# Reordering the opening and the first phase of a Mamba mixer: half of the step sizes under the down projection, four scores, B's and C's transposes and x's taps at other places

## The chip, the core and the metric

The kernel runs on one core of a Trainium2 chip. The core has five engines with a queue each, which run their instructions in order and wait for one another by semaphores: TensorE (PE; its weight loads are listed as PEld) for matmuls into the accumulation memory PSUM, VectorE (DVE) and ScalarE (ACT) for elementwise work, GpSimd (POOL) for elementwise work[...], and SyncE (SP), which here only issues the DMA transfers between the chip's main memory and the on-chip buffer. The metric is the device time of one execution in microseconds (us), lower is better.

## What is computed

Four residual blocks in a row on x, 1024 tokens of width 512 in two sequences of 512: a block-sparse linear layer, a gated feed-forward block (FFN) with dequantized weights, a Mamba-2 mixer, and the same FFN again. Each begins with a layer norm. The change is in the mixer and at the seam of the first FFN and the mixer. Cut to what matters (H = 128 heads of 64, 8 groups of B and C with 128 states, chunks of 128 tokens; the function's name is shortened):

```python
def mixer_ref(hidden_states, ...):
    proj = hidden_states @ in_proj_w.T          # gate 8192 | x 8192, B 1024, C 1024 | dt 128
    hBC = silu(causal_conv4(hBC) + conv_b)      # 4 taps along the tokens
    dt = jax.nn.softplus(dt + dt_bias)          # the step sizes
    A_dt = -jnp.exp(A_log) * dt
    x_dt = x * dt[..., None]
    A_cumsum = jnp.cumsum(Ac, axis=-1)          # within each chunk
    Lmat = jnp.exp(segment_sum(Ac))             # decay between two tokens of a chunk
    Gm = jnp.einsum('bclhn,bcshn->bclsh', Cch, Bch)
    M = Gm * Lmat                               # the scores
    Y_diag = einsum(M, x_dt)
    states = einsum(Bch * decay_states, x_dt)   # then carried from chunk to chunk
    Y_off = einsum(Cch, states) * exp(A_cumsum)
    y = (Y_diag + Y_off) + D * x
    y = y * rsqrt(mean(y * y) + EPS) * norm_w * silu(gate)
    return y @ out_proj_w.T
```

## The kernel before

**Order.** For PE, ACT and DVE the order of instructions is the order in which the program writes them; for POOL and SP a planner sets it from the same text, by what it expects to be ready. A small generator is the tool by which the text interleaves work: `seven` yields after each of seven products, and the caller puts other work between `next(steps)` calls.

**Projections.** A pair of 128-column weight tiles times all 1024 tokens is computed as a Strassen-like scheme, `seven` (L157): seven products instead of eight, each of two 128-deep steps of float32, 4 PE instructions. It needs sums of quarters of the tokens (`quarters`, L138, and `last_quarter`, L143: two subtractions on DVE, two on POOL, the last one in place) and sums of weight quarters (`left_sides`, four POOL instructions for each load of a pair). Its three PSUM banks x, y, z are written more than once: y by the second, fourth and sixth product. Between them DVE adds y to a temporary (L180, L185, L186, L194, L199), and the next product into y waits until that has read it. The finished quarters go to `done`, in the mixer to `conv` (L551): ACT writes bias and last tap (L553), and three DVE instructions, the taps (L556), are put on a list that `drain(n)` empties later. They read the PSUM bank, so it is in use until then.

**The seam.** The FFN ends with the down projection (L404): eight rows of 128 tokens, 28 PE instructions each. After each row, `to_mixer` (L1094) stores the row and starts its norm, and two rows later `turn` (L123) transposes it with four PE instructions into `xn_t`.

**The mixer's opening** (L777 on). `step_sizes` (L456) multiplies the tokens by the dt weights (`pre`, 32 PE instructions a sequence) and takes softplus in seven DVE and four ACT instructions over both sequences at once; `decays` (L503) makes the cumulative sums with a triangular matrix of ones, sends them to main memory (`acs_d`), and keeps copies and the chunk decays. The order of `before` on PE: step sizes of sequence 0, the last two tile transposes, step sizes of sequence 1, x of the first pair of tiles (seven products), B and C of group 0 (seven, in the banks of tag `yo`), `decays`, the gate of the first pair (seven). Then the silus.

**A phase** (L854) handles two tiles of 128 channels, 4 heads, in both sequences: four units (tile j, sequence b), of two heads each. It projects the next pair's x (`x_front`) and gate (`g_front`) while it finishes the present pair: `tokens` transposes x and multiplies by dt (L652, L656, and L660 on POOL), `group_scores` (L590; for a new group only) transposes B and makes C times B, masked, in `gm`; `scores` (L705) makes one head's exponentials of the sums (ACT: four L712, L719, L722) from a broadcast of `acs_d` (`load_sums`, L620), multiplies them by C on POOL (L723), and puts the multiplication by `gm` (L720, DVE) on a list that `flush` empties. `both_states` makes the states (L673 and five DVE instructions a unit), `half_scan` the outputs (L731, L740), `gated` (L750, L751) multiplies by the gate. `outs` multiplies the pair before last by the output weights (L765), eight times in a phase; phase 1 has nothing to multiply yet. Scores are numbered 0 to 7; two of the next pair's are made at the end of each phase, but in phase 1 of `before` all eight of the present pair are made in the phase itself. There are 31 such phases and a tail.

Of the kernel before, what the change touches and what calls it, by code (L numbers as in the profile page):

```python
# [24 lines left out]
G = 8  # L25
# [12 lines left out]
def kernel(  # L38
# [98 lines left out]

    def quarters():  # L138
        nc.vector.tensor_sub(tq[:, 0], B12, B11)
        nc.vector.tensor_sub(tq[:, 1], B22, tq[:, 0])  # L140
        nc.gpsimd.tensor_sub(tq[:, 2], B21, tq[:, 1])
# [177 lines left out]
    def ffn(which, first, waiting, after):  # L319
# [3 lines left out]
        with tc.tile_pool(name=f"ffn{which}", bufs=1) as pool:  # L323
# [80 lines left out]
            for t in range(NT):  # L404
                po = psum.tile([P, DIM], F32, tag="proj", name="ffn_o", bufs=3)
                for fc in range(NFC):
                    nc.tensor.matmul(  # L407
                        po,
                        lhsT=h_t[:, fc, t * P : (t + 1) * P],
                        rhs=down[:, fc, :],  # L410
                        start=(fc == 0),
                        stop=(fc == NFC - 1),
                    )
                nc.vector.tensor_add(x_sb[:, t, :], x_sb[:, t, :], po)
                after(t)


    def mixer(waiting):

        with ExitStack() as st:  # L420
# [13 lines left out]
            dt = sc.tile([P, NT, H], F32, tag="dt", name="dt")  # L434
            acs = sc.tile([P, NT, H], F32, tag="acs", name="acs")
# [9 lines left out]
            w_dt = weights()[:, :, 0, :]  # L445
            nc.sync.dma_start(
                w_dt, win_t[:, 2 * INTER + 2 * G * P :].rearrange("(kc p) h -> p kc h", p=P)
            )
            row = const.tile([P, 2, H], F32, name="row")
            dtb, aneg = row[:, 0, :], row[:, 1, :]  # L450
            nc.sync.dma_start(dtb, dt_bias.to_broadcast([P, H]))
            nc.sync.dma_start(aneg, a_log.to_broadcast([P, H]))
            nc.scalar.activation(aneg, aneg, AF.Exp)
            nc.vector.tensor_scalar(aneg, aneg, -1.0, None, ALU.mult)

            def step_sizes(wdt, pool):  # L456

                v = pool.tile([P, NT, H], F32, tag="bc", name="v", bufs=3)

                def pre(b):  # L460
                    pd = psum.tile([P, NCH, H], F32, tag="tr", name="pd")
                    for c in range(NCH):
                        t = b * NCH + c
                        for kc in range(KC):
                            nc.tensor.matmul(
                                pd[:, c, :],
                                lhsT=xn_t[:, kc, t * P : (t + 1) * P],
                                rhs=wdt[:, kc, :],
                                start=(kc == 0),
                                stop=(kc == KC - 1),  # L470
                            )
                    nc.vector.tensor_tensor(
                        v[:, b * NCH : (b + 1) * NCH, :],
                        pd,
                        dtb.unsqueeze(1).to_broadcast([P, NCH, H]),
                        ALU.add,
                    )

                e = pool.tile([P, NT, H], F32, tag="bc", name="e", bufs=3)
                u = pool.tile([P, NT, H], F32, tag="bc", name="u", bufs=3)
                pre(0)
                yield
                pre(1)
                nc.scalar.activation(e, v, AF.Abs)
                nc.scalar.activation(e, e, AF.Exp, scale=-1.0)
                yield
                nc.vector.tensor_scalar(u, e, 1.0, None, ALU.add)
                nc.vector.scalar_tensor_tensor(e, u, -1.0, e, ALU.add, ALU.subtract)  # L490
                nc.scalar.activation(dt, u, AF.Ln)
                nc.scalar.activation(u, dt, AF.Exp, scale=-1.0)
                yield
                nc.vector.tensor_mul(e, e, u)
                nc.vector.tensor_sub(dt, dt, e)
                nc.vector.scalar_tensor_tensor(dt, v, 0.0, dt, ALU.max, ALU.add)
                adt = pool.tile([P, NT, H], F32, tag="bc", name="adt", bufs=3)
                nc.vector.tensor_tensor(
                    adt, dt, aneg.unsqueeze(1).to_broadcast([P, NT, H]), ALU.mult
                )  # L500
                yield adt

            def decays(pool, adt):  # L503

                for b in range(2):
                    acs_t = room()
                    pt = psum.tile([H, SEQ], F32, tag="tr", name="pacs")
                    for c in range(NCH):
                        nc.tensor.matmul(
                            pt[:, c * P : (c + 1) * P],  # L510
                            lhsT=adt[:, b * NCH + c, :],
                            rhs=tri,
                            start=True,
                            stop=True,
                        )
                    nc.vector.tensor_copy(acs_t, pt)
                    nc.sync.dma_start(acs_d[:, b * SEQ : (b + 1) * SEQ], acs_t)
                for b in range(2):
                    cs = slice(b * NCH, (b + 1) * NCH)
                    pa = psum.tile([P, NCH, H], F32, tag="tr", name="pa")  # L520
                    pl = psum.tile([P, NCH, H], F32, tag="tr", name="pl")
                    nc.tensor.matmul(pa, lhsT=tri, rhs=adt[:, cs, :], start=True, stop=True)
                    nc.tensor.matmul(pl, lhsT=ones, rhs=adt[:, cs, :], start=True, stop=True)
                    nc.scalar.copy(acs[:, cs, :], pa)
                    nc.vector.tensor_tensor(
                        dec[:, b], pl[:, : NCH - 1], acs[:, b * NCH : (b + 1) * NCH - 1, :], ALU.subtract
                    )
                    nc.scalar.activation(dec[:, b], dec[:, b], AF.Exp)
                    nc.scalar.activation(e_last[:, b], pl[:, 1 : NCH - 1], AF.Exp)

            wrk = st.enter_context(tc.tile_pool(name="wrk", bufs=2))

            def load_pair(*cts):

                w = weights()
                if cts[1] == cts[0] + 1:
                    cols = slice(cts[0] * P, (cts[0] + 2) * P)
                    nc.sync.dma_start(
                        w, win_t[:, cols].rearrange("(kc p) (j c) -> p kc j c", p=P, c=P)
                    )  # L540
                else:
                    for j, ct in enumerate(cts):
                        nc.sync.dma_start(
                            w[:, :, j, :],
                            win_t[:, ct * P : (ct + 1) * P].rearrange("(kc p) c -> p kc c", p=P),
                        )
                return left_sides(w)
# [28 lines left out]

            def load_group(g):
                return load_pair(2 * NCT + g, 2 * NCT + G + g)
# [126 lines left out]
            def scores(ct, b, hh, bc, c_t, gm):  # L705

                h = 2 * ct + hh
# [12 lines left out]
                mults.append(lambda: nc.vector.tensor_mul(m, m, gm))  # L720
                ce = wrk.tile([P, NCH - 1, P], F32, name="ce", bufs=5)
                nc.scalar.activation(ce.rearrange("p c l -> p (c l)"), bc[:, hh, P:], AF.Exp)  # L722
                nc.gpsimd.tensor_mul(ce, ce, c_t[:, P:].rearrange("p (c l) -> p c l", l=P))  # L723
# [55 lines left out]
            wx = load_pair(NCT, NCT + 1)  # L779
            wbc = load_group(0)  # L780

            steps_dt = step_sizes(w_dt, wrk)
            next(steps_dt)
            while waiting:
                turn(waiting.pop(0))
            quarters()
            next(steps_dt)
            last_quarter()
            steps = x_front(0, wx, xcs)
            groups[0] = []  # L790
            steps_bc, made = group(0, wbc, "yo")
            next(steps)
# [3 lines left out]
            next(steps)  # L796
            drain(3)
            adt = next(steps_dt)
            run(steps)
            next(steps_bc)  # L800
            next(steps_bc)
            drain(3)
            next(steps_bc)
            next(steps_bc)
            drain(3)
            next(steps_bc)
            next(steps_bc)
            drain(3)
            run(steps_bc)
            wg = load_pair(0, 1)  # L810
            decays(wrk, adt)
# [5 lines left out]
            next(gate)  # L817
            for u in units:
                silu(xcs[u], xcs[u])
            next(gate)  # L820
            drain()
            run(gate)
            for b in range(2):
                for x in made[b]:
                    silu(x, x)
            for dst, src in later:
                silu(dst, src)
# [5 lines left out]
            heads = {}  # L833
            def half_scores(k, c, heads):

                j, b = units[k // 2]
                if k % 2 == 0:
                    heads[j, b] = []
                    heads["bc"] = load_sums(c + j, b)
# [312 lines left out]
```

## Time and profile before

| | us |
|---|---|
| median of 3 runs (lowest to highest) | 2351.61 (2350.02 to 2352.39) |
| the profiled execution | 2348.94 |
| its span | 2347.2 |
| down projection of the first FFN, from to | 220.5 to 318.7 |
| mixer's opening, to the first x transposes | 318.7 to 377.9 |
| phase 1, to the x transposes of phase 2 | 377.9 to 431.9 |
| phase 2, likewise | 431.9 to 480.9 |

The page gives, for each engine, busy time and its share of the span. PE is busy 98% of it. A group line names source line, engine and operation, result and inputs, shapes and count; then the busy time, the mean of one, and the idle time in front with what ended it. A line of the waits names the waiting instruction and what it waited for: us in total, times, longest. A line of the timeline has start, duration (of all merged instructions, from first start to last end), engine, line and operation, count, and in brackets the idle time in front. A line of the stretches has the stretch, its length, and for each engine busy time and count, in the order PE, PEld, DVE, ACT, POOL; then the granted PE clock, the DMA share and GB/s.

### The profile page before, as it was taken

The numbers are of one execution on the slowest core, as the hardware profiler recorded it, in microseconds if no ns is written. First come the engines' busy times: TensorE is split into PE (matmuls) and PEld (weight loads), VectorE is DVE, ScalarE is ACT, GpSimd is POOL, SyncE is SP. The second block draws the span as 40 slices with busy tenths as digits, with TensorE's granted clock in tenths as the row PEclk, the third lists the DMA queues.
The fourth block names the chain that finished last, engine by engine and source line by source line (L and its number), as shares of the span: only waits on it lengthen the run. The fifth ranks groups of instructions, "written<-read, shape, count | busy, mean of one in ns | idle before, by whom it ended". The sixth has DMA issues, their size and how long they took to land.

```text
span 2347.2 us, 27338 instructions
## 1 busy us (share of the span) xinstructions
PE 2296.7 (98%) x9626; PEld 1207.3 (51%) x9626; DVE 1614.6 (69%) x2802; ACT 1134.4 (48%) x2431; POOL 993.8 (42%) x963
## 2 busy tenths in 40 slices
PE   8999998999999999999999999999999999989999
PEld 4444444555555555555555545555555555544444
DVE  6454147878778788777777887878778788755520
ACT  2111025656665666556566556656665656521100
POOL 2763023434453544344445444434443544346500
PEclk9999999999999999999999999999999999999999
DMA  5662012222222222222222222222222221346500
GB/s 186 193 205 90 19 41 81 81 69 67 79 69 69 72 72 81 64 80 71 66 74 71 81 65 71 81 72 65 70 81 72 64 81 63 95 133 217 183 14 23
DMA packets 145576, 201.39 MB, mean 86 GB/s; under 512 B 6944, under 2 KB 91808, under 8 KB 145440
## 3 DMA queue, kind: packets, MB, share of 16 engines
q1 hardware_dynamic: 145440, 199.66, 27.1%
q8 instruction: 76, 1.25, 0.2%
q14 instruction: 60, 0.49, 0.1%
HBM read 194.91 MB, written 4.72 MB: 85 GB/s over the span
## 4 chain that ended last, share of the span: by engine, by line
PE 90%; DVE 8%; ACT 1%; issue 0%; DMA 0%; SPq 0%; DVEq 0%; ACTq 0%
PE proj L165 38%; PE po L765 18%; PE ffn_o L407 8%; PE yo L165 6%; PE py L731 4%; PE pst L673 4%; PE py L740 3%; PE x_tr L652 2%; DVE c_t L556 1%; DVE b_t L556 1%; DVE xc L556 1%; PE bs_o L294 1%; PE pg L357 1%; PE pu L357 1%; DVE m L720 1%; PE ln_tr L128 1%
## 5 line engine op out<-in xcount | busy, mean ns | idle before, releaser
L165 PE MATMUL proj<-xn_t,w 128*128 128x512 f32 x996 | 465.0, 598 | 7.6 <-ACT ce L722 7.0
L723 POOL TENSOR_TENSOR ce<-ce,c_t 128x384 f32<-128x384 f32 x256 | 269.9, 1058 | 453.9 <-ACT ce L722 451.6
L765 PE MATMUL po<-wo,gt 128*128 128x512 f32 x992 | 436.8, 595 | 0.0
L712 ACT ACTIVATE m<-bc,acs 128x128 f32<-128x128 f32 x1024 | 324.6, 389 | 8.9 <-PE py L731 8.9
L165 PE MATMUL proj<-tq,ws 128*128 128x512 f32 x664 | 309.5, 598 | 9.5 <-DVE xc L556 4.0
L765 PEld LDWEIGHTS po<-wo,gt 128*128 128x128 f32 x992 | 184.6, 190 | 219.6 <-issue 198.0
L165 PEld LDWEIGHTS proj<-xn_t,w 128*128 128x128 f32 x996 | 182.5, 191 | 207.2 <-issue 188.3
L720 DVE TENSOR_TENSOR m<-m,gm 128x512 f32<-128x512 f32 x256 | 220.2, 881 | 2.7 <-ACT m L719 2.7
L556 DVE SCALAR_TENSOR_TENSOR xc<-proj,cw,xc 128x511 f32<-128x511 f32 (+2 forms) x288 | 213.5, 742 | 2.5
L660 POOL TENSOR_TENSOR x_dec<-x_dt,dec 128x384 f32<-128x384 f32 x128 | 129.1, 1018 | 183.4 <-DVE x_dt L656 181.1
L165 PEld LDWEIGHTS proj<-tq,ws 128*128 128x128 f32 x664 | 122.4, 191 | 161.2 <-issue 142.7
L151 POOL TENSOR_TENSOR ws<-w 128x256 f32<-128x256 f32 x96 | 72.9, 759 | 309.2 <-DMA w<-in_win_t_dram 303.5
L407 PE MATMUL ffn_o<-down,h_t 128*128 128x512 f32 x448 | 193.4, 592 | 0.0
L775 DVE TENSOR_TENSOR x_sb<-x_sb,po 128x512 f32<-128x512 f32 x248 | 167.9, 678 | 24.6 <-PE po L765 24.0
L758 POOL TENSOR_TENSOR sq_acc<-sq_acc,y 128x512 f32<-128x512 f32 x128 | 176.3, 1391 | 17.1 <-ACT y L757 16.9
L731 PE MATMUL py<-m,x_dt 128*64 128x128 f32 x2048 | 181.0, 276 | 0.0
L719 ACT ACTIVATE m<-m 128x512 f32<-128x512 f32 x256 | 161.3, 630 | 7.4
L553 ACT ACTIVATE xc<-proj,cb,cw 128x512 f32<-128x512 f32 x96 | 71.2, 775 | 177.8 <-DVE proj L194 156.8
L165 PE MATMUL proj<-xn_t,ws 128*128 128x512 f32 x332 | 156.0, 592 | 0.0
L165 PE MATMUL proj<-tq,w 128*128 128x512 f32 x332 | 156.0, 592 | 0.0
L740 PE MATMUL py<-ce,state 128*64 128x128 f32 x1536 | 149.8, 273 | 0.0
L407 PEld LDWEIGHTS ffn_o<-down,h_t 128*128 128x128 f32 x448 | 84.7, 190 | 104.8 <-issue 104.8
(164 smaller groups left out, 3284.8 us busy)
## 6 DMA issues: line engine op xcount, KB each, us to landing
bc<-acs_d SPq DMA_DIRECT2D x128, 512.0 KB, 3.8
w<-in_win_t_dram SPq DMA_DIRECT2D x64, 512.0 KB, 3.9
wo<-in_wo_t_dram SPq DMA_DIRECT2D x31, 512.0 KB, 3.7
wi<-in_gate_w_dram SPq DMA_DIRECT2D x14, 512.0 KB, 4.0
zi<-in_gate_z_dram SPq DMA_DIRECT2D x14, 512.0 KB, 5.1
sf<-in_gate_s_dram SPq DMA_DIRECT2D x14, 512.0 KB, 5.1
wi<-in_up_w_dram SPq DMA_DIRECT2D x14, 512.0 KB, 4.9
zi<-in_up_z_dram SPq DMA_DIRECT2D x14, 512.0 KB, 5.9
```

The costliest lines, as they stand in the source:

```text
L165: nc.tensor.matmul(ps, lhsT=a[:, kc, :], rhs=b[:, kc, :], start=(start and kc == 0), stop=(stop and kc == KH - 1), skip_group_check=True,)
L407: nc.tensor.matmul(po, lhsT=h_t[:, fc, t * P : (t + 1) * P], rhs=down[:, fc, :], start=(fc == 0), stop=(fc == NFC - 1),)
L556: nc.vector.scalar_tensor_tensor(dst[:, s:], ps[:, : SEQ - s], cw[:, t, 3 - s : 4 - s], dst[:, s:], ALU.mult, ALU.add)
L712: nc.scalar.activation(m[:, c, :], bc[:, hh, c * P : (c + 1) * P], AF.Relu, bias=acs[:, t, h : h + 1], scale=-1.0,)
L719: nc.scalar.activation(m, m, AF.Exp, scale=-1.0)
L720: mults.append(lambda: nc.vector.tensor_mul(m, m, gm))
L723: nc.gpsimd.tensor_mul(ce, ce, c_t[:, P:].rearrange("p (c l) -> p c l", l=P))
L731: nc.tensor.matmul(py[hh * HD : (hh + 1) * HD, c * P : (c + 1) * P], lhsT=x_dt[:, c, hh, :], rhs=m[:, c, :], start=True, stop=(c == 0),)
L740: nc.tensor.matmul(py[hh * HD : (hh + 1) * HD, c * P : (c + 1) * P], lhsT=state[:, c - 1, hh, :], rhs=ce[:, c - 1, :], start=False, stop=True,
L758: nc.gpsimd.tensor_add(sq_acc[:, b, :], sq_acc[:, b, :], y)
L765: nc.tensor.matmul(po, lhsT=gts[j, b][:, c * P : (c + 1) * P], rhs=wo[:, j, :], start=(j == 0), stop=(j == PP - 1),)
L775: nc.vector.tensor_add(acc[:, t, :], acc[:, t, :], po)
```

## The change

No arithmetic changes, except that softplus is taken in two halves; the same work is written at other places.

- **Step sizes.** `step_sizes` takes one sequence and works in 512-wide rooms. Sequence 0's is put behind rows 5 and 6 of the down projection, with the load of the weights behind row 0; a last Sqrt brings that function's table back. `dt` and `acs` move to the pool that lives all the time. The first loads of x's, B's and C's weights are written behind rows 1 and 2.
- **Opening.** `decays` takes one sequence; sequence 0's stands at the start. Sequence 1's step sizes stand after x's first product, and `quarters` is cut in two parts. The order of the two POOL subtractions is turned round in the text. Sequence 1's `decays` stands between x and B, C.
- **Scores.** Scores 0 to 3 of phase 1 are made between the products of B and C; their multiplication by C (POOL) waits on a list until C is there (`ces`).
- **x's taps** are drained after x's fourth product and after the first, second and third of B and C (before: after x's fourth, and the second, fourth and sixth of B and C); B's and C's between the gate's first four, with one more batch ahead of the fourth.
- **Phase 1.** `group_scores` stands after x's first and second product, then the four masks; score 4 after the fourth product; all of x's taps are drained before the outputs of the first two units are gated; and the gate's seven products stand between scores 5 to 7, where later phases have `outs`. Phases from 2 on have their old order.

```diff
+    def two_quarters(s=slice(0, SEQ)):
+        nc.vector.tensor_sub(tq[:, 0, :, s], B12[:, :, s], B11[:, :, s])
+        nc.vector.tensor_sub(tq[:, 1, :, s], B22[:, :, s], tq[:, 0, :, s])
+
+    def third_quarter():
+        nc.gpsimd.tensor_sub(tq[:, 2], B21, tq[:, 1])
...
+    def step_sizes(b, wdt, dtb, aneg, rooms):
+        v, e, u = [r.rearrange("p (c h) -> p c h", h=H) for r in rooms]
+        cs = slice(b * NCH, (b + 1) * NCH)
+        d = dt[:, cs]
...
+            def decays(b):
...
+                nc.scalar.copy(acs_t, pt)
+                nc.sync.dma_start(acs_d[:, b * SEQ : (b + 1) * SEQ], acs_t)
+                pa = psum.tile([P, NCH, H], F32, tag="yo", name="pa", bufs=3)
+                pl = psum.tile([P, NCH, H], F32, tag="yo", name="pl", bufs=3)
...
+            wx, wbc = loaded
+            wg = load_pair(0, 1)
+            steps = x_front(0, wx, xcs)
+            decays(0)
+            turn(waiting.pop(0))
+            next(steps)
+            two_quarters(slice(0, SEQ - P))
+            turn(waiting.pop(0))
+            two_quarters(slice(SEQ - P, SEQ))
+            steps_dt = step_sizes(1, *step_args, [y_room() for _ in range(3)])
             next(steps_dt)
             last_quarter()
+            third_quarter()
             next(steps)
             next(steps_dt)
             next(steps)
             next(steps)
+            next(steps_dt)
             drain(3)
+            next(steps)
+            next(steps)
             run(steps)
+            decays(1)
+            groups[0] = []
+            ces = []
+            steps_bc, made = group(0, wbc, "yo")
             next(steps_bc)
+            half_scores(0, 0, heads, ces)
+            drain(3)
+            next(steps_bc)
+            drain(3)
+            half_scores(1, 0, heads, ces)
             next(steps_bc)
             drain(3)
             next(steps_bc)
+            half_scores(2, 0, heads, ces)
             next(steps_bc)
             next(steps_bc)
+            half_scores(3, 0, heads, ces)
             run(steps_bc)
             gate, later = g_front(wg, gts)
             next(gate)
             drain(3)
             next(gate)
             drain(3)
             next(gate)
+            drain(3)
             for u in units:
                 silu(xcs[u], xcs[u])
             next(gate)
             drain()
             for b in range(2):
                 for x in made[b]:
                     silu(x, x)
+            for f in ces:
+                f()
+            run(gate)
...
                 next(steps)
-                if ph == 1:
+                if not last:
                     group_scores(made, groups[0], [0])
-                    back_scores(0)
-                flush()
+                else:
+                    flush()
                 next(steps)
-                if ph == 1:
+                if not last:
                     group_scores(made, groups[0], [1])
                     made = None
-                    back_scores(1)
-                back_scores(2)
+                    flush()
+                else:
+                    back_scores(2)
...
                 flush()
+                if not last:
+                    back_scores(4)
                 both_states(0)
                 next(steps)
                 drain(3)
                 next(steps)
                 run(steps)
+                if not last:
+                    drain(3)
                 both_states(1)
-                finish(half_scan(units[:2]))
+                scans = half_scan(units[:2])
+                if not last:
+                    drain()
+                    gate, later = g_front(wg, gts_new)
+                finish(scans)
+
+                def between(k):
+                    if last:
+                        outs(k)
+                    else:
+                        next(gate, None)
+
                 for k in range(4):
-                    outs(2 * k)
+                    between(2 * k)
                     flush()
-                    back_scores(4 + k)
...
+                    if last or k:
+                        back_scores(4 + k)
...
+        def to_mixer(t, sg_tile):
             nc.sync.dma_start(x_d[t * P : (t + 1) * P, :], x_sb[:, t, :])
+            if t == 0:
+                state["args"] = step_weights()
+            if t in (1, 2):
+                state[t] = load_pair(NCT, NCT + 1) if t == 1 else load_group(0)
             if len(waiting_m) == 2:
                 turn(waiting_m.pop(0))
             waiting_m.append(norm_all(t))
+            if t == NCH + 1:
+                rooms = [sg_tile(*jb) for jb in ((0, 0), (0, 1), (1, 0))]
+                state["steps"] = step_sizes(0, *state["args"], rooms)
+                next(state["steps"])
+            if t == NCH + 2:
+                for _ in state["steps"]:
+                    pass
+                nc.scalar.activation(small.tile([P, 1], F32, name="root"), eps, AF.Sqrt)
```

## The prediction

> **What bounds the kernel now.** I read the page's busy shares first, then the waits of TensorE in the stretch that the change touches, then its timeline there, then the busy time by stretch. The page:
>
> ```profile
> PE 2296.7 (98%) x9626; PEld 1207.3 (51%) x9626; DVE 1614.6 (69%) x2802; ACT 1134.4 (48%) x2431; POOL 993.8 (42%) x963
> ```
>
> TensorE's list of matmuls is as long after the change as before, so the change can win only time in which TensorE waits or runs at a lower clock. The waits of TensorE between 319 and 470 us:
>
> ```profile
> PE proj L165 <- ACT ce L722: 7.0, 1, 7.0
> PE yo L165 <- DVE tmp L180: 4.0, 1, 4.0
> PE proj L165 <- DVE xc L556: 2.1, 1, 2.1
> PE x_tr L652 <- ACT b_tok L597: 1.3, 1, 1.3
> PE pa L522 <- DVE tmp L516: 0.7, 1, 0.7
> PE pl L523 <- ACT e_last L529: 0.6, 1, 0.6
> ```
>
> With three short ones (0.5, 0.5, 0.4) they make 17.1 us. The timeline of TensorE shows what follows a wait:
>
> ```profile
> 388.53 3.54 PE L165 MATMUL proj<-tq,ws 128*128 128x512 f32 x4
> ...
> 412.15 3.75 PE L165 MATMUL proj<-xn_t,w 128*128 128x512 f32 x4 [7.05 <-ACT ce L722]
> 415.69 2.00 PE L165 MATMUL proj<-tq,ws 128*128 128x512 f32 x4
> ```
>
> Four such instructions (one product of `seven`) take 1.72 us from start to start elsewhere; here 3.3 to 3.5, at half clock. Where the time goes, by stretch (columns: engine busy times, then the granted clock):
>
> ```profile
> 340.00:360.00 20.00, 15.99 (x40) 7.29 (x39) 15.97 (x20) 4.29 (x6) 4.75 (x4) 0.83 0.14 44
> 380.00:400.00 20.00, 18.23 (x70) 10.24 (x69) 11.11 (x21) 15.04 (x35) 11.02 (x12) 0.91 0.16 55
> 400.00:420.00 20.00, 10.84 (x78) 6.85 (x78) 19.65 (x37) 14.13 (x35) 11.65 (x11) 0.83 0.24 79
> ```
>
> In the last row VectorE is busy 19.65 of 20 while TensorE does 10.84: the end of phase 1 is bound by VectorE's in-order queue (taps, masks of scores, states, gating). Time lost in all: count from 318.71 (transposes after the last row of the down projection) to 432.74 (first product of phase 2), 114.0 us. The work in it at full clock: 35 products x 1.717 = 60.1; step sizes 2 x 3.58; sums and decays 5.4; x's transposes 2.6; B, C 2.4; states 2.6; outputs 6.4; three tile transposes 1.3: 88 us. So 26 us are lost, and that is the ceiling.
>
> **The parts that cost nothing.** Sequence 0's step sizes: 32 PE instructions (3.58 us) only change place. Its DVE part, 0.69 + (0.80+1.63+1.22+1.23+1.63+1.63)/2 = 4.8 us, its ACT part, 2.1 us, and seven table loads of 1.28 lie beside rows of the down projection, 12.02 us each, in which DVE waits 9.7 us and ACT 10.9. Bare they would cost the 4.8. The six loads moved with them (step weights, two rows, x's pair, two for B and C) were issued at 194.8 to 219, before that projection, and still are. The cumulative sums' copies go from DVE (2 x 0.68) to ACT.
>
> **The new order, walked.** I write down each engine's list in the new order and let each instruction start when its engine and inputs are free, by the durations of the trace: tap 0.75, add 0.69, score 2.25 on ACT (four of 0.33 apart, 0.54, 0.42), mask 0.8 (rows of 0.68 to 1.75, mean 0.98 with POOL beside it), PE result to reader 0.2. Zero is again the end of the last row.
>
> Opening: sums of sequence 0 to 3.15, tile transposes, first product to 5.3; the second step sizes wait 0.4 (ACT's copies stand behind an Exp table load) and end at 9.7. POOL does the last quarter (2.38) to 12.1 and the third (2.36) to 14.5; their products start at 13.2 and 16.6, so both are hidden, barely. x ends at 20.0, the old 4.0 wait being gone: DVE has half the softplus left. B's and C's second product then waits 0.85: it needs the bank of sequence 1's sums (`pa`), whose copy stands on ACT behind x's last conv copies (22.5 to 24.1) and the copy of the transposed sums (24.6), and ends at 25.2. Nine taps are now drained ahead of C's adds (L185, L186): 25.8 + 9 x 0.75 + one add of 0.7, so DVE reaches them at 33.3, and the sixth product, which writes the bank that the first add reads, waits 1.75 (32.3 to 34.05). Four scores (9.0 us of ACT) fill ACT's queue between these products; behind them stand the conv copies and the gate's first copy (42.2), so the gate's adds come at 42.9 and 48.1 and its sixth product waits 1.0. The gate ends at 52.3. A clock at half rate behind the 1.75 would cost nothing here, since ACT and DVE set the later times. Add the moved 3.58: 55.9 against 59.2 before, **3.3 won**.
>
> Phase 1: x's transposes and B's, C's, to 59.1, all that reads a gate bank having been released by DVE at 52.4 or ACT at 55; from 60.0 DVE runs without pause: four masks (3.2), x_dt (1.3), adds (1.3), states (2.2), three taps, adds, three taps, states, six taps (to 80.4), two outputs (2.9), one mask, the gate's add at 84.9. TensorE gets past both outputs at 74.9 and starts the gate, where the old order had nothing for it; its second product waits 1.9 for taps that still read its PSUM bank, the third 0.45, the fourth 2.55 for that add. The gate ends at 91.8, the last two outputs wait for the last mask (94.1) and end at 95.7. Then a new stall: x's transposes of phase 2 wait for ACT, whose second new score needs a buffer that the outputs free at 93.4: 2.25 + table 1.28 + silu 0.6, so 97.7, a wait of 2.0 on nothing else. First product at 98.7, with the 3.58 102.3: **11.7 won** of the 114.0.
>
> **The clock after a wait.** [...] the pair of waits of 1.28 and 0.49 us at 386 to 388 was followed by a product at 3.3 us, while a wait of 2.11 at 417.7 was not. I therefore charge only waits of near 2 and more: the 2.55 and the 2.0 with about six and five in ten, at 1.7 us each, 1.9 together (bounds 0 and 5.1, if all three slow a product that nothing covers). **9.8 won**.
>
> **The table load.** Two loads are on the path (before the second step sizes, before phase 2). [...] the last of four ACT instructions (L712) ended at 384.12, the load ran from 384.14, and the Exp behind it started at 385.43. I take 1.28.
>
> **Bounds of what the trace can't show.** SP's and POOL's orders are made by a planner. If POOL takes the gate's weight sums ahead of the third quarter, they wait for a load issued at 9.7 and landing 4.3 later (issue 327.98, first sum 332.28), then 3 to 5 us: x's sixth product waits 2 to 5. Against that, if x's third quarter goes first, 0.4. I take nothing. Masks at 0.68 would give 1 us back, at 1.14 take 3. Later phases keep their order: zero, within 1 us.
>
> **Sum.** The profiled execution took 2348.94 (span 2347.2); minus 9.8, 2339.1. The median of the runs stands 2.7 above it, so 2351.6 - 9.8 = 2341.8.
>
> **Rivals.**
> *All the waits go.* If ACT and DVE run ahead of my walk (no waits on the adds in the gate), 15 to 18 of the 26 are won: about 2335. For: DVE is idle for some 7 us of the opening and the first part of phase 1. Against: the run of DVE from 60 to 85 has no gap.
> *VectorE takes it back.* Each wait is replaced by one on DVE's queue: masks at 1.14, the weight sums ahead of the third quarter, three slow products: 3 + 3 + 3 off: 1 to 4 left, about 2349. For: 19.65 of 20 busy. Against: the same work sits in more time.
> *The sums of sequence 1 come late: slower.* The third score, at 35.5 in ACT's queue, reads a broadcast that goes out to DRAM at 24.6 and back: issue to issue 2.1 (361.36 to 363.45), landing 3.8 median, 6.5 at most, so about 31. If the planner puts weight loads whose buffers come free only when B and C end (39.2) ahead of it on SP, it lands at 43 to 48, and the conv copies, the gate's first copy and all behind them are late by 8 to 12.5. The change loses from 45.3 on; at 48 it is 2354. Against: the scores stand ahead of those loads in the text.
>
> **How the numbers follow.** Main case 0.55 (own range 2338 to 2346), all waits 0.15, VectorE 0.22, late sums 0.08. Range 2334.5 to 2349.5: it leaves out about 0.06 below, and the tail of VectorE's case and most of the late sums above. The bound of 0.2% is 4.7 us, about what a measurement of this kernel tells from no change. Faster: 0.55 + 0.15 + 0.08 of VectorE's case; same: 0.14 + 0.03; slower: 0.05 of the late sums.
>
> **What would show it.** Right: no wait of 7 us on a score and no 4.0 on `tmp`; waits of 2 to 3 us on taps and on the gate's add in phase 1; a wait near 2 us ahead of phase 2's transposes; phase 2's first product about 10 us earlier. Wrong: ACT waiting for `bc` in the opening, POOL's third quarter behind weight sums, or a granted clock below 0.9 through the new phase 1.

## The result and the profile after

The changed kernel takes **2341.61 us** (median of 5 runs, 2340.76 to 2344.64), the kernel before 2351.02 in the same comparison (2350.02 to 2352.39): a ratio of 0.9965, 95% interval 0.9955 to 0.9976. The medians differ by 9.4 us, the recorded ratio says 8.2 (5.6 to 10.6); so one us between two kernels below is not settled by their medians alone. The profiled execution took 2340.76 us with a span of 2339.0. The medians of the kernel before moved between 2349.1 and 2351.0 from one group of runs to the next, so every kernel below is compared with the runs of before that went with it.

The page's busy shares of the changed kernel:

```profile
PE 2295.3 (98%) x9626; PEld 1206.3 (52%) x9626; DVE 1612.8 (69%) x2808; ACT 1143.3 (49%) x2444; POOL 991.1 (42%) x963
```

The same 9626 matmuls, and nearly the same work on every engine. The waits of TensorE from 318 to 470 us:

```profile
PE proj L171 <- DVE gt L186: 3.2, 2, 2.8
PE x_tr L645 <- ACT xc L567: 2.1, 1, 2.1
PE proj L171 <- DVE gt L191: 1.3, 1, 1.3
PE yo L171 <- DVE tmp L191: 1.3, 1, 1.3
PE proj L171 <- DVE xc L552: 1.3, 2, 1.1
PE pd L467 <- ACT xn_t L129: 0.7, 1, 0.7
PE yo L171 <- ACT acs L536: 0.4, 1, 0.4
```

With two of 0.3 they make 10.9 us, against 17.1 before. The waits of 7.0 on a score and of 4.0 on `tmp` are gone; shorter ones stand in their place, where the walk of the prediction had put them. The timeline of TensorE at the end of the stretch:

```profile
407.91 5.12 PE L171 MATMUL proj<-xn_t,w 128*128 128x512 f32 x8 [2.76 <-DVE gt L186]
...
422.30 1.18 PE L645 MATMUL x_tr<-ident,xc 128*128 128x128 f32 x8 [2.11 <-ACT xc L567]
423.31 1.88 PE L171 MATMUL proj<-xn_t,w 128*128 128x512 f32 x4
```

The eight instructions behind the wait of 2.76 took 5.12 us, and 3.60 to 3.70 elsewhere: 1.5 lost to half clock. The four behind the wait of 2.11 ran at full clock. Counted from the tile transposes behind the last row of the down projection (322.97), phase 2's first product comes at 100.3; before it came at 114.0. The 3.58 us of step sizes that left the stretch are in that difference, so 10.1 us are won. The stretches that answer to those shown of before:

```profile
340.00:360.00 20.00, 18.23 (x48) 8.07 (x47) 16.34 (x24) 11.54 (x26) 3.62 (x6) 1.00 0.36 118
...
380.00:400.00 20.00, 19.57 (x126) 12.42 (x124) 17.57 (x40) 7.04 (x13) 7.82 (x11) 1.00 0.10 27
400.00:420.00 20.00, 15.91 (x80) 8.12 (x80) 13.65 (x20) 12.45 (x33) 7.79 (x8) 0.91 0.25 79
```

The clock is full in the first two (0.83 and 0.91 before), and VectorE no longer fills the last one.

### The profile page after: what moved, and what is told of

It reads as the page before. It is cut to its first block, busy times and chain, and to the rows that moved or that the text cites. A ratio compares the mean times of both kernels' runs of the same rounds, so it can differ in the third digit from the quotient of the medians.

```text
span 2339.0 us, 27347 instructions
## 1 busy us (share of the span) xinstructions
PE 2295.3 (98%) x9626; PEld 1206.3 (52%) x9626; DVE 1612.8 (69%) x2808; ACT 1143.3 (49%) x2444; POOL 991.1 (42%) x963
## 4 chain that ended last, share of the span: by engine, by line
PE 90%; DVE 7%; ACT 1%; issue 1%; DMA 1%; POOL 0%; SPq 0%; DVEq 0%
PE proj L171 38%; PE po L768 19%; PE ffn_o L413 8%; PE yo L171 6%; PE py L734 4%; PE pst L666 4%; PE py L743 3%; PE x_tr L645 2%; DVE c_t L552 1%; DVE b_t L552 1%; PE bs_o L300 1%; DVE xc L552 1%; PE pg L363 1%; PE pu L363 1%; PE pgm L596 1%
## 5 line engine op out<-in xcount | busy, mean ns | idle before, releaser
L761 POOL TENSOR_TENSOR sq_acc<-sq_acc,y 128x512 f32<-128x512 f32 x128 | 175.4, 1384 | 17.1 <-ACT y L760 16.9
L734 PE MATMUL py<-m,x_dt 128*64 128x128 f32 x2048 | 182.2, 276 | 0.1
L734 PEld LDWEIGHTS py<-m,x_dt 128*64 128x64 f32 x2048 | 123.7, 137 | 29.4 <-issue 19.0
```

Source lines behind the costliest of these rows:

```text
L734: nc.tensor.matmul(py[hh * HD : (hh + 1) * HD, c * P : (c + 1) * P], lhsT=x_dt[:, c, hh, :], rhs=m[:, c, :], start=True, stop=(c == 0),)
L761: nc.gpsimd.tensor_add(sq_acc[:, b, :], sq_acc[:, b, :], y)
```

## The experiments

All kernels were measured against the kernel before. "Opening" runs from the tile transposes to the first transposes of x in phase 1, plus 3.6 us where sequence 0's step sizes lie outside; "phase 1" from there to phase 2's first product. Both are from one profiled execution; "half" counts the windows of 3.41 us at half clock in these two stretches; one cost up to 1.7 us (3.54 for 1.88, at 388.53 of before), and their number can differ between executions (the granted clock of the runs of before went from 0.992 to 0.996; last section); "won" is the difference of the medians of the runs.

| kernel | opening | phase 1 | half | median | won |
|---|---|---|---|---|---|
| before | 59.2 | 54.8 | 5 | 2351.02 | |
| changed | 55.8 | 48.1 | 1 | 2341.61 | 9.4 |
| e1 scores back | 54.3 | 48.8 | 0 | 2340.52 | 9.6 |
| e2 gate back | 55.8 | 45.6 | 1 | 2338.05 | 12.1 |
| e3 step sizes back | 62.9 | 48.2 | 3 | 2346.94 | 3.2 |
| e4 gate's add first | 55.6 | 44.9 | 0 | 2337.76 | 12.4 |
| e7 more VectorE work | 55.5 | 48.4 | 0 | 2341.57 | 7.7 |
| e10 gate and scores back | 54.4 | 49.3 | 2 | 2339.26 | 10.0 |
| e11 gate and taps back | 55.5 | 48.4 | 2 | 2339.57 | 9.7 |
| e12 new phase 1 alone | 58.3 | 50.1 | 2 | 2346.51 | 2.7 |
| e13 new opening alone | 54.3 | 51.8 | 2 | 2342.65 | 6.5 |
| e8 add and silus first | 55.8 | 42.3 | 0 | 2334.82 | 14.3 |
| e14 the same, scores back | 54.5 | 46.9 | 0 | 2338.99 | 10.1 |
| e9 e8 with the opening's taps back | 54.2 | 42.4 | 0 | 2333.29 | 16.6 |

**e1: the first four scores back in phase 1** (masks still behind both groups' `gm`).

```diff
-            half_scores(0, 0, heads, ces)
...
-            half_scores(3, 0, heads, ces)
...
+                    back_scores(0)
...
+                    back_scores(1)
+                    back_scores(2)
...
-                if last:
-                    back_scores(3)
+                back_scores(3)
```

> The changed kernel with scores 0 to 3 of phase 1 made in phase 1 again (0 behind the group's first part, 1 and 2 behind its second, 3 behind x's third product); the step sizes, the taps and the gate stay as changed. Theory (the early scores take ScalarE's work out of the stage in which VectorE waits for it): the masks wait for score 2, which ends about 3.5 us later than the masks start now, and x's token products, the adds and the taps stand behind them; the opening wins about 1 us because no scores stand ahead of the gate's first copy. Phase 2's first product 3 to 5 us later than in the changed kernel, 2344 to 2347 us. Rival (VectorE's sum of work alone sets phase 1, and the scores' place does not matter): within 1 us of the changed kernel's 2341.6.

Measured: 2340.52 us, ratio 0.9961 (0.9946 to 0.9976). The opening is 1.5 us shorter and phase 1 0.7 longer. The theory's forecast fell, but part of its mechanism is there: the masks wait for scores (0.6 and then 1.55 us), as VectorE's timeline shows,

```profile
385.88 0.69 DVE L715 TENSOR_TENSOR m<-m,gm 128x512 f32<-128x512 f32 x1 [1.55 <-ACT m L714]
```

and TensorE's wait on the taps behind them is 2.19 for 1.05. What the delay meets is a later wait: the one on the gate's add is 2.04 for 2.76, and no half clock follows it (the eight instructions behind it took 3.70), where the changed kernel lost 1.5. So in these executions the early scores are worth nothing; at an equal clock they would be worth some 0.7 (an estimate: 1.5 and 0.7 in phase 1 against 1.5 in the opening).

**e2: phase 1's gate back behind the outputs.**

```diff
-                    if last:
-                        outs(k)
-                    else:
-                        next(gate, None)
+                    outs(k)
...
-                if last:
-                    gate, later = g_front(wg, gts_new)
+                gate, later = g_front(wg, gts_new)
+                if not last:
+                    next(gate)
+                    next(gate)
+                    next(gate)
```

> The changed kernel with phase 1's gate at its old place: three products ahead of the last two outputs, four behind them, its adds on VectorE behind the masks of scores 4 to 7; the early step sizes, scores and taps stay as changed. Theory (my walk: the waits of phase 1 come from VectorE's order, not from TensorE having nothing to do): the add of the gate comes behind four masks at about 87 us after the down projection, but the product that needs it now stands behind the outputs and ends in time; x's transposes find their silus done, so the wait of 2.1 us there is gone too. 3 to 5 us faster than the changed kernel, 2337 to 2339. Rival (the gate's products between the scores are what won the time): the idle stretch comes back, at least half of the 7.0 us, 2345 to 2349.

Measured: 2338.05 us, ratio 0.9954 (0.9937 to 0.9971): 3.6 us below the changed kernel's median (2.7 by the column "won"), 2.6 of them in the stretch, with one window at half clock in each (in e2 from 407.61 to 410.4, where one instruction of L734 took 0.42 for 0.27). The gate's wait of 2.76 and the one of 2.11 on ACT are gone; of the waits of this kernel one is of that size:

```profile
PE py L734 <- DVE m L715: 2.8, 1, 2.8
```

So interleaving the gate with masks and gating costs time where it stands.

**e3: sequence 0's step sizes back behind the projection.** Sequence 0's part beside the projection goes, but for the last Sqrt, which now stands behind row 0; `step_sizes(0, ...)` stands where `decays(0)` stood, its later parts behind x's second and fourth product, and `decays(0)` just ahead of `decays(1)`.

```diff
-            decays(0)
+            old_rooms = [wrk.tile([P, 2, SEQ], F32, tag="bc", name="v", bufs=3)[:, 0, :] for _ in range(3)]
+            steps_0 = step_sizes(0, *step_args, old_rooms)
+            next(steps_0)
...
             run(steps)
+            decays(0)
             decays(1)
```

> The changed kernel with sequence 0's step sizes in the opening again, in the same halves, and both sequences' cumulative sums behind x's products. Theory (the move takes 4.1 us of VectorE's and 2.1 us plus two table loads of ScalarE's work out of an opening in which x's chain waits for VectorE): 2.5 to 4 us slower than the changed kernel, 2344 to 2346, with TensorE waiting for the sums' inputs. Rival (VectorE had room in the opening, and halving plus the rest of the order did it): 0 to 0.5 us, 2341.6 to 2342.

Measured: 2346.94 us, ratio 0.9988 (0.9981 to 0.9994), 5.3 slower than the changed kernel, more than forecast. The opening is 7.1 longer; most of that is a wait that the change undone doesn't explain, with some 2.7 of half clock behind it (2.08 for 1.02 at 352.01, 3.56 for 1.88 at 353.88). Of the waits of this kernel:

```profile
PE pl L535 <- ACT acs L536: 4.4, 1, 4.4
```

Both calls of `decays` stand together here and want four banks of a tag with three. This placement can't price the moved step sizes; their share of the opening's gain stays open.

**e4: the gate's first two products, and with them its first add, ahead of gating units 0 and 1.**

```diff
                     gate, later = g_front(wg, gts_new)
+                    next(gate)
+                    next(gate)
                 finish(scans)
```

> The changed kernel with one step of phase 1 turned round: the gate's first two products, and with them its first add, stand ahead of the gating of units 0 and 1 and of the mask of score 4 in VectorE's queue. Theory: the fourth product's wait of 2.76 us and the half clock behind it (1.5 us) go, its sixth waits about 0.4; phase 2's first product 4 us earlier, 2337 to 2338.5. Rival (the same work still stands ahead of the last masks, so the wait moves to the last two outputs): under 1 us, 2340.6 to 2341.6.

Measured: 2337.76 us, ratio 0.9949 (0.9934 to 0.9964). The wait of 2.76 and the half clock behind it are gone (3.60 for 5.12), phase 2's first product comes 3.4 us earlier, and the theory held: TensorE's fourth gate product hung on the add's place in VectorE's list.

**e7: four more multiplications on VectorE behind the first four masks** (on tiles not read again).

```diff
+                    spare = [made[b][0] for b in range(2)]
                     made = None
                     flush()
+                    for _ in range(2):
+                        for x in spare:
+                            nc.vector.tensor_mul(x, x, x)
```

> The changed kernel with four more multiplications of 128x512 on VectorE (about 0.68 us each, 2.7 in all, on tiles that nobody reads again) behind the four masks of the first scores in phase 1: extra work, the output is not touched. My theory: from there to the gate's first add VectorE has no gap, and that run sets TensorE's fourth gate product and with it the end of the stretch. Then the wait on the add in phase 1 grows from 2.8 to about 5.4 and phase 2's first product comes 2.4 to 2.8 us later: near 2344.2 us. Rival: another engine sets that end (ACT with the new scores): less than 0.7 us later, near 2342.

Measured: 2341.57 us, ratio 0.9967 (0.9956 to 0.9979), the changed kernel's time. The theory's forecast fell and the rival's time came, but not for the rival's reason. VectorE's timeline of the changed kernel, and then VectorE's and TensorE's of this one:

```profile
387.00 0.69 DVE L191 TENSOR_TENSOR tmp<-tmp,proj 128x512 f32<-128x512 f32 x1 [0.58 <-PE proj L171]
...
407.18 0.67 DVE L186 TENSOR_TENSOR gt<-gt,proj 128x512 f32<-128x512 f32 x1
```

```profile
385.27 2.49 DVE L938 TENSOR_TENSOR b_t<-b_t 128x512 f32<-128x512 f32 x4
...
408.95 0.67 DVE L186 TENSOR_TENSOR gt<-gt,proj 128x512 f32<-128x512 f32 x1
```

```profile
409.68 3.70 PE L171 MATMUL proj<-xn_t,w 128*128 128x512 f32 x8 [2.76 <-DVE gt L186]
```

From the zero point (322.97 and 323.40) the add starts at 84.2 and at 85.6: of 2.49 us of work 1.3 reach it. The rest fills VectorE's gap of 0.58, and here the masks start 0.3 earlier, with a shorter opening. TensorE first waits 1.4 for x_dt, so its outputs of units 0 and 1 come 1.3 later as well, and the wait on the add is 2.76 in both; but here full clock follows it, 3.70 against 5.12. The delay was real, and in this execution the clock gave it back. Whether it is in the median can't be told: 1.3 us lie within the intervals of the two ratios.

**e10 and e11: what of phase 1's change is left with the gate back.** e10 is e1 and e2 together; left are the masks' place, score 4 early and the taps. e11 is e2 with the last nine taps between the outputs' masks again:

```diff
-                if not last:
-                    drain(3)
...
-                if not last:
-                    drain()
...
-                    if last:
-                        drain(1 if k < 3 else 0)
+                    drain(1 if k < 3 else 0)
```

> Of the new phase 1 only three things stay: the masks of the group ahead of the flush, score 4 taken early, and all taps of x drained ahead of the gating of y. The scores 0 to 3 stand in phase 1 again and the gate stands behind the outputs again. If the opening and the taps' place win, and interleaving the gate and the early scores win nothing: opening near 50.7, phase 1 near 46.3 (45.6 of the kernel with the gate back, and 0.7 for the scores), first product of phase 2 at 97.0, 3.3 us ahead of the changed kernel: about 2338.3. Rival: with the scores and the gate both back, ACT's queue is as late as before and the wait of 7 us on a score returns: phase 1 near 54.8, first product at 105.5, about 2346.8.

> The kernel with the gate back at its old place, and the last nine taps of x again between the outputs, each behind a mask that waits for a score of ACT; the early scores stay. My theory: VectorE's taps then stand behind masks that wait for ACT, x's copies behind the taps come late, and TensorE waits for them or for ACT behind them: 2 to 5 us slower than the kernel with the gate alone back (2338.05), 2340 to 2343. Rival: with four scores early, ACT is ahead of the masks and the place of the taps is worth nothing: 2337 to 2339.

Measured: e10 2339.26 us, ratio 0.9958 (0.9943 to 0.9973); e11 2339.57, ratio 0.9959 (0.9945 to 0.9973). e10 lies between its two forecasts, and shows what e1 did not: with the gate back, the early scores win 3.7 us of phase 1 (49.3 against 45.6) for 1.4 of the opening; some 1.6 of the 3.7 are the second window at half clock, which e2 has not. For e11 the theory's mechanism held. Of its waits:

```profile
PE proj L171 <- ACT ce L717: 5.3, 1, 5.3
```

The wait on a score returns, a product at half clock follows it (3.75 for 1.88 at 402.89), and phase 2's first product is 2.5 us later than in e2; in the medians it is 1.5, somewhat under the 2 to 5 forecast. The taps' place has worth with the gate back. Taps between the masks with the gate interleaved were not tried: there VectorE would wait for a product that itself waits for taps behind it.

**e12 and e13: each stage alone.** e12 is the kernel before with e1's phase 1; e13 is e1 with phase 1 as it was before.

> The opening of the kernel before (both step sizes behind the projection, cumulative sums last, nothing of the scores early) with the new phase 1 alone, scores 0 to 3 in it. If opening and phase 1 add up: 59.2 of before and 48.8 of the kernel with the scores back, first product of phase 2 at 108.0 against 114.0, 6.0 us won: about 2344.1. Rival: the new phase 1 only works since the new opening leaves its engines ahead: less than 2 us won, above 2348.

> The new opening alone (sequence 0's step sizes beside the projection, the cumulative sums inside it, no early scores) with phase 1 as it was before. If opening and phase 1 add up: 50.7 to phase 1, with the moved 3.58 54.3 against 59.2, so 4.9 us won: about 2344.8 against some 2349.7 of before. Rival: phase 1 of before, with its wait of 7 us on a score, takes the gain back, since ACT's scores start no earlier against VectorE's taps: less than 1.5 us won, above 2348.2.

Measured: e12 2346.51 us, ratio 0.9988 (0.9981 to 0.9994), 2.7 won; e13 2342.65, ratio 0.997 (0.9959 to 0.9982), 6.5 won. The two add up to 9.2, and e1, which has both, won 9.6. But they don't divide as forecast. In e12 the first product came as computed (108.4 for 108.0), but 1.5 were lost ahead of the stretch, and 1.8 in phase 2. In e13 more is won in the stretch than the opening's 4.9: phase 1, with its code untouched, is 3.0 shorter, though its largest wait is still there:

```profile
PE proj L171 <- ACT ce L717: 7.0, 1, 7.0
PE proj L171 <- DVE xc L552: 1.6, 1, 1.6
```

The timelines of TensorE in the first part of phase 1 say where, of before (the product at 388.53 with its 3.54 us is shown in the prediction) and of e13:

```profile
386.89 0.66 PE L652 MATMUL x_tr<-ident,xc 128*128 128x128 f32 x4 [1.28 <-ACT b_tok L597]
388.04 0.66 PE L652 MATMUL x_tr<-ident,xc 128*128 128x128 f32 x4 [0.49 <-DVE gm L604]
```

```profile
380.64 0.66 PE L645 MATMUL x_tr<-ident,xc 128*128 128x128 f32 x4 [0.78 <-ACT b_tok L590]
381.79 0.66 PE L645 MATMUL x_tr<-ident,xc 128*128 128x128 f32 x4 [0.49 <-DVE gm L597]
382.28 1.88 PE L171 MATMUL proj<-tq,ws 128*128 128x512 f32 x4
```

One wait is 0.5 shorter, and the half clock behind it, 1.7 us, is gone; a wait of 0.5 at 379.46 in before is gone too. That makes 2.7 of the 3.0, and 1.7 of it is clock.

**e8, e14, e9: towards a better kernel.** e8 is e4 with the second new score behind the silus of x. e14 is the same on e1. e9 is e8 with x's taps in the opening in three lots of three, as before.

```diff
                 finish(scans)
-                half_scores(1, c0, heads_new)
                 if last:
+                    half_scores(1, c0, heads_new)
                     next(gate)
...
                 for dst, src in later:
                     silu(dst, src)
+                if not last:
+                    half_scores(1, c0, heads_new)
```

> The kernel with the gate's first add ahead of the gating of units 0 and 1 (2337.76), and with the silus of x ahead of ACT's second new score. My theory: the wait of 2.4 us of phase 2's x transposes on ACT is a real end of the stretch, so it goes and nothing else takes its place: 1.5 to 2.4 us faster, 2335.4 to 2336.3. Rival: the second new score is then late for phase 2's masks or the gate's last add ends the stretch at the same time: within 0.8 us of 2337.8.

> The same two edits on the kernel with the scores 0 to 3 back in phase 1, where the opening was 1.5 us shorter. My theory: the opening's gain stays (50.7 against 52.0) and phase 1 loses 0.7 for the scores: 0.5 to 1 us faster than with the early scores, 2334.5 to 2335.8. Rival: with the gate's add early, ACT's four scores in phase 1 are late for the first masks and VectorE's whole line moves back: 2337 or more.

> The kernel with the first add and the silus of x ahead (2334.82), and in the opening x's taps in three lots of three behind the second, fourth and sixth product of B and C, as the kernel before had them, in place of nine between the second and the fourth. My theory: the nine taps ahead of C's first add are what the sixth product of B and C waits 1.3 us for, so with them later that wait goes and the opening ends 0.5 to 1.3 us earlier: 2333.5 to 2334.3. Rival: VectorE and ACT set the opening's end either way, and only the place of the wait moves: within 0.4 us of 2334.8, or later, since the last taps then stand behind the gate's first add.

Measured: e8 2334.82 us, ratio 0.9936 (0.9921 to 0.9951); e14 2338.99, ratio 0.9951 (0.9936 to 0.9966); e9 2333.29, ratio 0.9927 (0.9913 to 0.994). e8 went as the theory had it, a little better. In e14 the theory fell and the rival held: the first masks wait for ACT, as they do in e1. VectorE's timeline:

```profile
385.93 0.69 DVE L715 TENSOR_TENSOR m<-m,gm 128x512 f32<-128x512 f32 x1 [1.55 <-ACT m L714]
```

TensorE's wait on the taps is 2.19 here too, for 1.05 in the changed kernel. With less of a later wait to hide this, and no half clock in either kernel, the early scores are worth 3.3 us net (phase 1 and opening of e8 and e14: 98.1 against 101.4). e9 went as its theory had it, a little better: no wait on `tmp` in the opening, which is 1.6 shorter. Its largest waits from 318 to 470 us:

```profile
PE proj L171 <- DVE gt L191: 1.3, 1, 1.3
PE proj L171 <- DVE xc L552: 1.3, 2, 1.1
PE py L734 <- DVE m L715: 1.0, 1, 1.0
```

e9 is faster than both kernels: 16.6 us against before. Its 8.3 us against the changed one (7.2 by "won") are 7.4 in the stretch (92.9 against 100.3 to phase 2's first product).

## Why the prediction was right

**The sum** was 2341.8 and the median is 2341.61; that they agree to 0.2 us is luck. The stretch won 10.1 for 9.8. Outside it two terms were off, and they cancel. The span fell by 8.2, not 9.8: 0.7 were lost in the kernel's first matmuls, long before the stretch, and 1.2 in later phases and at the end, where one more window at half clock (2056.0 to 2059.4) lies. And the median stands 0.85 above the profiled execution (2340.76), not 2.7. That the step sizes beside the projection cost nothing held: the tile transposes behind it come 4.26 later, which is the moved 3.58 and the 0.7 lost before.

**Where the 10.1 come from.** Nearly half is clock, by the durations of TensorE's products: half clock cost the stretch 6.3 us before (2.75 at 349.12, 1.66 at 388.53, 1.87 at 412.15) and 1.5 after. The prediction counted the 114.0 of before as they were and its walk at full clock, so this is inside its sum, but it doesn't say that so much of the gain is clock.

**The opening**: 3.4 won for 3.3. "The second step sizes wait 0.4" was 0.66; x ended at 21.0 for 20.0; the second product of B and C waited 0.44 for 0.85, the sixth 1.32 for 1.75, the gate's sixth 1.34 for 1.0, and the gate ended at 52.2 for 52.3. POOL took the third quarter first, the order that the prediction had as its alternative at 0.4; the wait was 0.27 (TensorE at 336.98). Of the 4.0 by which waits and half clock shrank, 2.75 are the two products that together took 6.35 us in before, at 349.12: two thirds were clock.

**Phase 1**: outputs of units 0 and 1 ended at 74.9 for 74.9, the gate's add at 84.9 for 84.9 too, and the fourth gate product waited 2.76 for 2.55. The waits of 1.9 and 0.45 on taps were 1.05 and 0.27; the one on x's silus 2.11 for 2.0.

**The clock charge**: 1.9 for two waits. One was followed by half clock (1.5), one not. As a mean it was well placed; e7, with the same two waits, shows that none need follow.

**The table load** at 1.28: of the two loads on the path, ACT's timeline of the changed kernel has one at 326.83 and the Exp behind it at 328.12, the other at 420.32 and the silu at 421.62: 1.29 and 1.30 from start to start. ACT's work ended 0.02 us or less before each load.

**Where the reasons were wrong.** "TensorE gets past both outputs at 74.9 and starts the gate, where the old order had nothing for it" was told as phase 1's gain. e2 puts the gate back and is faster, so the walk was right and the reason wrong: the interleaved gate hangs on the add behind gating and mask. And the prediction split the gain as the code is split, 3.3 and 6.5. In the changed kernel the stages show that split (3.4 and 6.7), but 3.0 of phase 1's part comes with the new opening alone (e13; 1.7 of it clock), and the new phase 1 adds 3.0 behind that opening, with the scores where they were (e1). "From 60.0 DVE runs without pause" left out a gap of 0.58, which took up part of e7's extra work.

None of the rivals came: no wait on `bc` in the opening; VectorE's stretch fell from 19.65 busy to 13.65; "all the waits go" needed e8's two moves, and its 2335 is what e8 measured.

## What to carry to other kernels

The largest wait in a list is not the largest gain: with the wait of 7.0 us still in place e13 won 6.5, and e1, which also removes it, 9.6. When a wait is broken up, ask for each new one what stands ahead of the releasing instruction on its engine; moving one add ahead of gating and a mask that TensorE didn't wait for yet (e4), and one score behind silus that it did wait for (e8), won 6.8 us more by the medians, 5.8 in the stretch. Price an edit in company: the early scores cost 0.8 us in the stretch here, where half clock hid what they won, and were worth 3.3 once the later waits were gone. And count the windows at half clock on both sides before a difference of some us is put down to an edit: of the 10.1 us here, 4.8 are clock (6.3 before, 1.5 after).

## What the hardware showed

**Half clock came in windows of one grid.** In the traces of before and of the changed kernel, from 20 us on to the last instruction, the stretches of half clock are 3.413 us long or two or three times that, and within each trace their starts lie whole multiples of 3.413 apart (before: 347.65, 388.61, 409.09 and 2050.90, 12, 6 and 481 of them; changed: 407.39, 2042.37 and 2056.02, 479 and 4). Whether half clock came was here a matter of the idle time in the one window before it, not of the length of a wait. The stretches of the changed kernel, cut on its grid, and of e7 around its wait on the add (the first number behind the comma is TensorE's busy time, the third from the right the clock):

```profile
403.97:407.38 3.41, 1.17 (x3) 0.19 (x1) 3.38 (x5) 3.36 (x9) 1.03 (x2) 1.00 0.43 147
407.39:410.80 3.41, 2.89 (x4) 1.35 (x5) 0.46 (x1) 3.13 (x8) 3.41 (x4) 0.50 0.42 154
```

```profile
404.59:408.00 3.41, 2.07 (x5) 0.68 (x4) 3.34 (x5) 3.36 (x10) 2.00 (x2) 1.00 0.42 154
408.00:411.41 3.41, 1.73 (x4) 0.87 (x5) 1.63 (x3) 3.37 (x9) 2.28 (x3) 1.00 0.32 117
411.42:414.83 3.41, 3.41 (x9) 1.52 (x8) 2.36 (x3) 0.92 (x2) 2.13 (x2) 1.00 0.10 37
```

The same wait of 2.76 us leaves 2.24 of one window idle in the first, and half clock follows; in e7 it lies across the first two stretches, which are idle for 1.34 and 1.68, and the clock stays full. In the changed kernel the wait of 2.11 lies across two windows of the grid (from 417.63 and from 421.04, idle for 0.95 and 1.26), and nothing follows.

From 20 us on, the windows at full clock that half clock followed were idle for 1.78, 2.09, 2.53 and 3.41 us in before (from 385.20, 2047.49, 344.24 and 405.68) and for 2.08, 2.18 and 2.24 in the changed kernel (from 2038.96, 2052.61 and 403.97). Of those that it did not follow, the idlest had 2.00 and 1.64 in before (from 2061.15 and 415.92) and 1.34 in the changed kernel (from 369.84). So in these two traces both occur between 1.78 and 2.00. Windows already at half clock were followed by another with 1.24 to 3.24 idle (1.47 at 347.65 of before, 1.24 at 2045.79 of the changed kernel), and by full clock with 0.65 and less.

So the wait of 2.76 us cost 1.5 more in the changed kernel and nothing more in e7, and two short ones in one window (1.28 and 0.49 in before, 1.78 idle in all) were followed by 1.66 lost. The runs of before spread with the clock: in the mean, the eight with a granted clock of 0.992 took 2352.2 us, the thirteen with 0.996 2347.9.
